# The third LSTM by seven block products, single groups by seven products too, and nine work tiles

## The chip, the cores and the metric

The kernel runs on one core of one Trainium2 chip. The metric is the device time of one execution in microseconds (us). The engines of the core are TensorE (PE, matmuls; PEld is its loading of weights), VectorE (DVE), ScalarE (ACT), GpSimd (POOL) and SyncE (SP), which here only issues transfers. All arithmetic is in f32.

## The reference, cut to what matters

The input is `x` of 128 x 64 x 256 (128 graphs of 64 nodes, 256 features) with one 64 x 64 adjacency matrix. Four layers follow one another, each with a residual and a layer norm: three graph convolutions; a spectral layer with the eigenvectors of the graph's Laplacian; a layer with two graph convolutions and four LSTMs; and a masked attention. The change is in the four LSTMs of the third layer:

```python
for p in range(1, MAX_SKIP + 1):                 # p = 1, 2, 3, 4
    nw = Tv // p                                 # 64 // p windows of p nodes
    wins = h[:, :nw * p, :].reshape(Bv * nw, p, Hd)
    last = _lstm_last(Wih[p - 1], Whh[p - 1], bih[p - 1], bhh[p - 1], wins)
    idx = jnp.arange(nw) * p + (p - 1)
    h = h.at[:, idx, :].set(last.reshape(Bv, nw, Hd))
```

One step of an LSTM is `x_t @ Wih.T + h @ Whh.T + bias`, four gates i, f, g, o of 256 features each, then `c = sigmoid(f) * c + sigmoid(i) * tanh(g)` and `h = sigmoid(o) * tanh(c)`. The first step has h = 0 and c = 0, so it needs neither `Whh` nor the gate f. LSTM p works on windows of p nodes and replaces the last node of each, so LSTM 3 sees what LSTM 2 wrote, and LSTM 4 what LSTM 3 wrote.

## The kernel before

**Groups and units.** The 128 graphs are 16 groups of eight graphs, 512 rows of 256 features each. Layer 0 (the first part, up to about 845 us) runs over all groups first, with the eigenvectors computed beside it. The other three layers then run group by group. `unit` (L1663) is the work of a unit: the first twelve groups make six units of two groups (pairs), the last four (`SINGLE = 4`) one unit each. `UNITS = 4` units are under way at a time.

**The planner.** Layers 1 to 3 are written as notes to a planner, `Plan` (L104). Each note is an operation (or a few matmuls) on one engine with a cost in us; `Plan.run` (L164) keeps a clock for each engine and emits the operation that can start first, among those within 0.02 us the one with the earliest due time. The due time is the group's number times `PERIOD` less the longest remaining chain of the operation. That sets the order of instructions on each engine, which then is fixed. The cost of a matmul is given in `products` (L1237): 1.673 ns a moving column plus 3 ns, at least 0.223 us. All instructions are issued in one helper, L162, so the profile puts them on that line, and they are told apart by tiles.

**Tiles.** Buffers come from named sets of slots: eight PSUM banks (`ps`), `WIDE` = 7 work tiles `w` of 1024 columns, `NARROW` = 3 of 512 (`v`), `GATES` = 6 gate tiles of 1024 columns, `CELLS` = 3 for the cell state `c`, `OUTS` = 4 for `hs`, the output handed to the next step. A tile is taken when its first operation is emitted and comes free when its last one is done. `Plan.MOST` (L112) tells how many slots are kept for the oldest unit.

**The LSTMs.** `to_lstm` (L1320) makes `hT`, the group's 512 rows with features on the partitions, as two `w`-sized halves k of 64 nodes x 8 graphs. A gate's weights are 256 x 256: two contraction halves k by two output halves h, so 128 x 128 blocks.

- `lstm` (L1483) is the direct form: for every gate and output half it sums over k the products of a 128 x 128 block and n moving columns, n being 8 graphs x number of windows. With p = 3 it has n = 8 x 21 = 168, with p = 4 n = 8 x 16 = 128. A first step has 3 gates x 2 halves x 2 = 12 matmuls, a later one 4 x 2 x 4 = 32.
- `fast` (L1540) is the form with seven products: the moving columns are cut in two halves w of n columns each, so that a gate is a product of 2 x 2 blocks, and seven products of blocks stand for the eight (Winograd's form of Strassen's method). A first step has 7 x 3 = 21 matmuls of n columns, a later one 7 x 4 x 2 = 56, where the direct form would have 24 and 64 of n columns. It needs four sums of weight blocks, made once by `add_weights` (L1216) on DVE into tiles `sums`, four sums of moving blocks per input (T1 to T4, on DVE, in a `w` tile), and three copies (ACT) and three additions (DVE) from PSUM in each pass over the gates. If (number of gates) x n is over 512, the gates are done in two passes of two. `quarters` (L1209) gives the four blocks of the weights.

LSTM 1 (`singles`, n = 256) and LSTM 2 (`pairs`, n = 128) use `fast` for every group, the halves being the first and last 32 nodes. LSTM 3 is `lstm(hT, 3, 0, 21)` for every group. LSTM 4 is `four` for a pair (L1648, n = 128, the halves being the two groups), and `lstm(hTs[0], 4, 0, 16)` for a single group.

The three lines that say which form LSTM 4 takes:

```python
        if len(groups) == 2:
            four(hTs)
        else:
            lstm(hTs[0], 4, 0, 16)
```

Of the kernel before, what the change touches and what calls it, by code (L numbers as in the profile page):

```python
# [11 lines left out]
F32 = mybir.dt.float32  # L12
AF = mybir.ActivationFunctionType
ALU = mybir.AluOpType
# [738 lines left out]
P = 128  # L753
D = 256
# [3 lines left out]
WIDE = 7  # L758
# [3 lines left out]
CELLS = 3  # L762
OUTS = 4
LASTS = 3
PERIOD = 17.0
# [62 lines left out]
def kernel(  # L828
# [25 lines left out]
    nc = tc.nc  # L854
# [6 lines left out]
    def tl(pool, shape, tag, **kw):  # L861
        uid[0] += 1
        return pool.tile(shape, F32, tag=tag, name=f"{tag}_{uid[0]}", **kw)
# [11 lines left out]
    def load(pool, name, src, pattern, shape, **kw):  # L875
        t = pool.tile(shape, F32, name=name)
        nc.sync.dma_start(t, src.rearrange(pattern, **kw))
        return t
# [88 lines left out]
    def run(out, pairs):  # L967
        for i, (lhsT, rhs) in enumerate(pairs):
            mm(out, lhsT, rhs, i == 0, i == len(pairs) - 1)
# [204 lines left out]
    wih, whh = [], []  # L1174
    for i in range(4):
        wih.append(load(wb, f"wih{i}", c_ih[i], "(k p) f -> p k f", [P, 2, 1024], p=P))
        whh.append(load(wb, f"whh{i}", c_hh[i], "(k p) f -> p k f", [P, 2, 1024], p=P) if i else None)
# [31 lines left out]
    def quarters(w):  # L1209
        w = w.rearrange("p k (q h m) -> p k q h m", q=4, h=2)  # L1210
        return [w[:, k, :, h] for h in range(2) for k in range(2)]

    ways = {}
    SPARE21 = {(1, 0), (2, 0), (2, 1)}

    def add_weights(p, ready):  # L1216
        ways[p] = []
        names = "igo" if p == 1 else "ifgo"
        for k, w in enumerate((wih[p - 1], whh[p - 1])):
            if w is None:  # L1220
                continue
            spare21 = (p, k) in SPARE21
            s = wb.tile([P, 4 - spare21, len(names), P], F32, name=f"sums{p}{k}")
            s, w = plan.tile("sums", [P, 4 - spare21, len(names), P], s), plan.tile("sums", [P, 2, 1024], w)
            whole = quarters(w)
            for at, to in ((slice(0, 1), slice(0, 1)), (slice(2, 4), slice(1, 3))) if p == 1 else ((slice(0, 4),) * 2,):
                a11, a12, a21, a22 = (x[:, at] for x in whole)
                S1, S2, S4, S3 = [s[:, j, to] for j in range(4 - spare21)] + [a21] * spare21
                V.tensor_add(S1, a21, a22, ready=ready)
                V.tensor_sub(S2, S1, a11, ready=ready)  # L1230
                V.tensor_sub(S4, a12, S2, ready=ready)
                V.tensor_sub(S3, a11, a21, ready=ready)
            raw = [{q: x[:, "ifgo".index(q)] for q in names} for x in whole]
            sums = [{q: s[:, j, i] for i, q in enumerate(names)} for j in range(4 - spare21)] + [raw[2]] * spare21
            ways[p].append([raw[0], raw[1], raw[3], sums[0], sums[1], sums[3], sums[2]])

    def products(calls, also=(), **kw):  # L1237

        size = lambda x: x.at.size if isinstance(x, Part) else int(np.prod(x.shape[1:]))
        cost = sum(max(0.001673 * size(c[2]) + 0.003, 0.223) for c in calls)  # L1240
        plan.note("PE", [("matmul", (o, l, r), {"start": a, "stop": z, **kw}) for o, l, r, a, z in calls], cost,
                  also=also)
# [8 lines left out]
    def work():  # L1251
        return plan.tile("w", [P, 1024])
# [4 lines left out]
    def ps4(shape=(P, 512)):  # L1257
        return plan.tile("ps", shape)
# [61 lines left out]
    def to_lstm(xs, there):  # L1320
# [20 lines left out]
        lstm(hT, 3, 0, 21)  # L1341
# [141 lines left out]
    def lstm(hT, p, first, nw):  # L1483

        n = 8 * nw
        wi, wh, bias = wih[p - 1], whh[p - 1], cbi[:, p - 1, :]
        hs = None
        for t in range(p):  # L1490
            rows = slice(first + t, first + t + (nw - 1) * p + 1, p)
            xt = [hT[:, k, rows, :] for k in range(2)]
            last = t == p - 1
            names = "figo" if t else "igo"
            gate = []
            for h in range(2):
                G = plan.tile("gates", [P, 1024])[:, :len(names) * n].rearrange("p (q n) -> p q n", n=n)
                gate.append({q: G[:, i] for i, q in enumerate(names)})
            if not t:
                c = plan.tile("c", [P, 512])[:, :2 * n].rearrange("p (h n) -> p h n", h=2)  # L1500
            new = None if last else plan.tile("hs", [P, 512])[:, :2 * n].rearrange("p (h n) -> p h n", h=2)
            for h in range(2):
                for q in names:
                    j = 2 * "ifgo".index(q) + h
                    m = slice(j * P, (j + 1) * P)
                    pp = ps4()[:, :n]
                    ins = [(wi[:, k, m], xt[k]) for k in range(2)]
                    outs = [(wh[:, k, m], hs[:, k, :]) for k in range(2)] if t else []
                    if t and h == 0 and q in names[:2]:

                        run(pp, ins, last=False)
                        run(pp, outs, first=False)
                    else:
                        run(pp, ins + outs)
                    S.activation(gate[h][q], pp, AF.Tanh, bias=bias[:, j:j + 1], scale=0.5 if q == "g" else 0.25)
                    if q == "g":
                        to = gate[h]["g"] if t else c[:, h, :]
                        if t:
                            V.scalar_tensor_tensor(c[:, h, :], gate[h]["f"], 1.0, c[:, h, :], op0=ALU.add,
                                                   op1=ALU.mult)  # L1520
                        V.scalar_tensor_tensor(to, gate[h]["i"], 1.0, gate[h]["g"], op0=ALU.add,
                                               op1=ALU.mult)
                        if t:
                            V.scalar_tensor_tensor(c[:, h, :], c[:, h, :], 0.5, to, op0=ALU.mult, op1=ALU.add)
                        S.activation(gate[h]["i"], c[:, h, :], AF.Tanh, scale=0.5)
                    if q == "o" and not last:
                        V.scalar_tensor_tensor(new[:, h, :], gate[h]["o"], 1.0, gate[h]["i"], op0=ALU.add,
                                               op1=ALU.mult)
            if p == 4 and t == 2:
                plan.late = plan.ops[-1]  # L1530
            if last:

                for h in range(2):
                    V.scalar_tensor_tensor(hT[:, h, slice(first + p - 1, first + nw * p, p), :],
                                           gate[h]["o"].rearrange("p (w b) -> p w b", b=8), 1.0,
                                           gate[h]["i"].rearrange("p (w b) -> p w b", b=8), op0=ALU.add,
                                           op1=ALU.mult)
            hs = new

    def fast(p, n, x, hs=None, c=None, new=None, write=None):  # L1540
# [8 lines left out]
        def parts(v):  # L1549
            return v.rearrange("p (r b) -> p r b", b=8)  # L1550
# [11 lines left out]
        T = work()[:, :4 * n * len(ins)].rearrange("p (s i n) -> p s i n", s=len(ins), i=4)  # L1562
        T1, T2, T3, T4 = ([parts(T[:, s, i]) for s in range(len(ins))] for i in range(4))
# [60 lines left out]
    def state(tag):  # L1624
        return plan.tile(tag, [P, 512]).rearrange("p (h w n) -> p h w n", h=2, w=2)

    def turn_out(dst, o, t):
        V.scalar_tensor_tensor(dst, o.rearrange("p (r b) -> p r b", b=8), 1.0, t.rearrange("p (r b) -> p r b", b=8),
                               op0=ALU.add, op1=ALU.mult)
# [18 lines left out]
    def four(hTs):  # L1648

        def write(h, o, t):  # L1650
            for w in range(2):
                turn_out(hTs[w][:, h, 3:64:4, :], o[:, w], t[:, w])

        c, hs = state("c"), None
        for t in range(4):
            x = [[hTs[w][:, k, t:t + 61:4, :] for w in range(2)] for k in range(2)]
            new = state("hs") if t < 3 else None
            fast(4, 128, x, hs, c, new, write)
            if t == 2:
                plan.late = plan.ops[-1]  # L1660
            hs = new

    def unit(groups):  # L1663

        if groups[0] == 0:
            add_weights(1, 10.0)
            add_weights(2, 30.0)
            add_weights(4, 60.0)
# [17 lines left out]
        if len(groups) == 2:  # L1686
            four(hTs)
        else:
            lstm(hTs[0], 4, 0, 16)
# [11 lines left out]

    spare[0] = lambda: tl(few, [P, D], "spare")
# [56 lines left out]
```

## Time and profile before

| What | Value |
|---|---|
| median of 3 runs | 2364.02 us (2361.47 to 2365.95) |
| the profiled execution's own time | 2365.63 us |
| its span, first to last instruction | 2363.8 us |
| TensorE clock granted, mean | 0.992 |
| PE busy | 2313.2 us (98%), 19872 matmul passes |
| PEld busy | 2035.5 us (86%), 19872 weight loads |
| DVE busy | 1630.6 us (69%), 5562 instructions |
| ACT busy | 1137.4 us (48%), 2838 instructions |
| POOL busy | 142.8 us (6%) |
| PE's share of the chain that ended last | 92% |

A busy PE is not PE at its peak, since the lengths of matmuls overlap. The lines of a group read: line, engine, operation, output tile <- inputs (moving, then weights), shape of the weights, shape of the moving data, count | busy us, mean ns | idle time of the engine before them, and who ended it.

### The profile page before, as it was taken

The page shows a single profiled execution, that of the slowest core. Times are in us where ns is not written, and L with a number is a line of the kernel's source. Part 1 is how long each engine was busy: PE and PEld are TensorE (multiplying, and loading weights), DVE is VectorE, ACT ScalarE, POOL GpSimd, SP SyncE. Part 2 cuts the span into 40 slices and gives each one's busy share as a digit, 9 for nine tenths or more (in the row PEclk, how much of TensorE's full clock was granted, in tenths as well). Part 3 has the DMA queues.
Part 4 walks back from the last instruction along what each step waited for, and adds up shares of the span by engine and source line. Part 5 has one row for each costly group of instructions (what it writes and reads, how often), then busy time and mean ns, then how long its engine had stood idle before and what let it go on. Part 6 is the DMA issues. An engine that isn't in the chain of part 4 may idle for free.

```text
span 2363.8 us, 50357 instructions
## 1 busy us (share of the span) xinstructions
PE 2313.2 (98%) x19872; PEld 2035.5 (86%) x19872; DVE 1630.6 (69%) x5562; ACT 1137.4 (48%) x2838; POOL 142.8 (6%) x315
## 2 busy tenths in 40 slices
PE   8999999999999999999999999999999999999996
PEld 6877888887787778999899899899999998998995
DVE  6888887778898557558567666756755858567535
ACT  2333343333333346555546545545556455545544
POOL 0000000000000010001000100100000101011002
PEclk9999999999999999999999999999999999999998
DMA  7000000000000040002111211220210312222001
GB/s 236 10 1 10 19 10 10 10 10 10 11 10 10 1 161 13 16 11 72 54 42 55 81 51 39 80 65 32 81 43 32 120 48 66 66 92 84 19 1 48
DMA packets 79837, 108.08 MB, mean 46 GB/s; under 512 B 23280, under 2 KB 63984, under 8 KB 79600
## 3 DMA queue, kind: packets, MB, share of 16 engines
q1 hardware_dynamic: 79248, 104.58, 13.3%
q8 instruction: 156, 2.56, 0.4%
q14 instruction: 81, 0.66, 0.1%
q10 hardware_dynamic: 352, 0.28, 0.0%
HBM read 57.90 MB, written 45.09 MB: 44 GB/s over the span
## 4 chain that ended last, share of the span: by engine, by line
PE 92%; DVE 5%; ACT 1%; issue 1%; POOL 0%; DMA 0%; SPq 0%; ACTq 0%; POOLq 0%; DVEq 0%
PE ps L162 60%; PE ps L963 30%; PE ps L1006 2%; DVE D L52 1%; DVE X L162 1%; PE pc L312 1%; DVE w L162 1%; DVE tw L52 0%; DVE st L162 0%; POOL rs L162 0%; DVE gates L162 0%; ACT gates L162 0%; DVE ss L52 0%; DVE v L162 0%; DMA XA<-in_x_dram 0%
## 5 line engine op out<-in xcount | busy, mean ns | idle before, releaser
L162 PE MATMUL ps<-w,wih 128*128 128x128 f32 (+2 forms) x3708 | 649.7, 299 | 3.2 <-DVE gates L162 1.7
L162 PEld LDWEIGHTS ps<-w,wih 128*128 128x128 f32 x3708 | 550.6, 191 | 33.0 <-issue 13.6
L162 ACT ACTIVATE gates<-ps,cbi 128x168 f32<-128x168 f32 (+2 forms) x722 | 261.5, 388 | 207.7 <-PE ps L162 204.1
L162 PE MATMUL ps<-w,sums 128*128 128x128 f32 (+1 forms) x2368 | 353.8, 289 | 3.0 <-ACT gates L162 2.0
L162 PE MATMUL ps<-hs,whh 128*128 128x128 f32 (+1 forms) x1952 | 343.2, 291 | 1.4 <-DVE hs L162 1.4
L162 PEld LDWEIGHTS ps<-w,sums 128*128 128x128 f32 x2368 | 307.6, 192 | 16.6 <-issue 4.3
L162 PEld LDWEIGHTS ps<-hs,whh 128*128 128x128 f32 x1952 | 288.3, 191 | 3.2 <-DVE hs L162 1.8
L162 ACT ACTIVATE gates<-gates,cbi 128x256 f32<-128x256 f32 (+2 forms) x500 | 214.3, 477 | 129.1 <-DVE gates L162 129.0
L162 DVE TENSOR_TENSOR gates<-gates,ps 128x512 f32<-128x512 f32 (+2 forms) x264 | 157.5, 601 | 164.1 <-PE ps L162 157.1
L963 PE MATMUL ps<-aw,h 128*128 128x256 f32 x1024 | 228.2, 380 | 0.0
L963 PEld LDWEIGHTS ps<-aw,h 128*128 128x128 f32 x1024 | 192.6, 190 | 25.9 <-issue 0.4
L162 ACT COPY gates<-ps 128x512 f32<-128x512 f32 (+2 forms) x264 | 136.8, 520 | 160.6 <-PE ps L162 158.8
L972 ACT ACTIVATE h<-h 128x512 f32<-128x512 f32 x128 | 80.6, 630 | 184.4 <-DVE h L52 184.2
L162 DVE SCALAR_TENSOR_TENSOR gates<-gates 128x256 f32<-128x256 f32 (+3 forms) x188 | 78.4, 418 | 69.9 <-ACT gates L162 69.6
L963 PE MATMUL ps<-aw,m 128*128 128x512 f32 x256 | 120.5, 612 | 0.9 <-ACT m L1010 0.9
L963 PE MATMUL ps<-m,aw 128*128 128x256 f32 x512 | 119.7, 387 | 1.0 <-ACT LV L385 0.6
L963 PE MATMUL ps<-ss,tw 128*128 128x256 f32 x512 | 117.8, 379 | 0.1
L963 PE MATMUL ps<-ss,aw 128*128 128x256 f32 x512 | 116.7, 379 | 0.0
L963 PEld LDWEIGHTS ps<-m,aw 128*128 128x128 f32 x512 | 98.1, 194 | 17.3 <-issue 3.0
L162 DVE SCALAR_TENSOR_TENSOR c<-gates,c 128x256 f32<-128x256 f32 (+2 forms) x156 | 56.6, 363 | 76.8 <-ACT gates L162 76.4
L963 PEld LDWEIGHTS ps<-ss,aw 128*128 128x128 f32 x512 | 96.8, 190 | 13.0
L162 POOL TENSOR_SCALAR rs<-mv 128x2 f32<-128x2 f32 x96 | 23.7, 256 | 1390.8 <-DVE mv L162 1372.1
(326 smaller groups left out, 3559.2 us busy)
## 6 DMA issues: line engine op xcount, KB each, us to landing
far<-w SPq DMA_DIRECT2D x42, 512.0 KB, 2.7
w<-far SPq DMA_DIRECT2D x168, 128.0 KB, 3.0
X<-rest SPq DMA_DIRECT2D x24, 512.0 KB, 3.3
out_dram<-X SPq DMA_DIRECT2D x64, 128.0 KB, 1.8
rest<-XA SPq DMA_DIRECT2D x12, 512.0 KB, 2.6
rest<-X SPq DMA_DIRECT2D x12, 512.0 KB, 2.8
XA<-in_x_dram SPq DMA_DIRECT2D x22, 256.0 KB, 6.0
wih<-in_c_ih_dram SPq DMA_DIRECT2D x4, 1024.0 KB, 7.7
```

What stands on the lines that cost most here:

```text
L52: return getattr(self.engine, name)(out, *args, **kw)
L162: getattr(e, name)(*[real(x) for x in args], **{k: real(v) for k, v in kw.items()})
L312: PE.matmul(out, lhsT, rhs, start=True, stop=True)
L963: PE.matmul(out, lhsT, rhs, start=start, stop=stop)
L972: S.activation(dst, src, AF.Relu)
L1006: PE.matmul(p[h][m, k, t, :], src[hs, t, f], sqT2[hs, hs], start=True, stop=True)
```

## The change

LSTM 3 goes to `fast` too, and LSTM 4 does so for single groups. A new function `long` takes the place of `four` and serves both LSTMs and both kinds of unit: for a pair the halves are the two groups; for a single group they are windows 0 to 7 and 8 to 15 (p = 4), or graphs 0 to 3 and 4 to 7 (p = 3, where 21 windows can't be halved). n is 64 // p x 4 for each group of the unit: 168 and 128 for a pair, 84 and 64 for a single group. `lstm` goes away. LSTM 3 leaves `to_lstm` and runs in `unit` when all the unit's groups have come through LSTM 2.

`add_weights` makes sums for p = 3 too. The fourth weight sum of every LSTM now overwrites the block a21 that it is made from, so a `sums` tile holds three. LSTM 1's weights are loaded in the order i, g, o without f, in two transfers. A `fast` step whose T1 to T4 do not fit in one `w` tile takes two. The spare output of the norms left over from layer 0 goes to a part of the `sums` tile of LSTM 4. The slots become `WIDE` 9, `CELLS` 2 (state tiles are 672 columns instead of 512), `OUTS` 2, `PERIOD` is 18, and the planner's cost of a matmul 1.673 ns a column + 10 ns, without a least value.

```diff
-WIDE = 7
+WIDE = 9
 NARROW = 3
 GATES = 6
 ATT = 2
-CELLS = 3
-OUTS = 4
+CELLS = 2
+OUTS = 2
 LASTS = 3
-PERIOD = 17.0
+PERIOD = 18.0
...
-        wih.append(load(wb, f"wih{i}", c_ih[i], "(k p) f -> p k f", [P, 2, 1024], p=P))
+        if i:
+            wih.append(load(wb, f"wih{i}", c_ih[i], "(k p) f -> p k f", [P, 2, 1024], p=P))
+        else:
+            wih.append(wb.tile([P, 2, 768], F32, name="wih0"))
+            for to, at, n in ((0, 0, 256), (256, 512, 512)):
+                nc.sync.dma_start(wih[0][:, :, to:to + n],
+                                  c_ih[0].rearrange("(k p) f -> p k f", p=P)[:, :, at:at + n])
...
+            nq = len(names)
+            s = wb.tile([P, 3, nq, P], F32, name=f"sums{p}{k}")
+            if p == 4:
+                spare[0] = lambda s=s: s[:, 0, 0:2, :].rearrange("p q n -> p (q n)")
+            s, w = plan.tile("sums", [P, 3, nq, P], s), plan.tile("sums", [P, 2, nq * 2 * P], w)
+            a11, a12, a21, a22 = whole = quarters(w)
+            S1, S2, S4 = (s[:, j] for j in range(3))
+            V.tensor_add(S1, a21, a22, ready=ready)
+            V.tensor_sub(S2, S1, a11, ready=ready)
+            V.tensor_sub(S4, a12, S2, ready=ready)
+            V.tensor_sub(a21, a11, a21, ready=ready)
...
-        cost = sum(max(0.001673 * size(c[2]) + 0.003, 0.223) for c in calls)
+        cost = sum(0.001673 * size(c[2]) + 0.01 for c in calls)
...
-        lstm(hT, 3, 0, 21)
         return hT
...
-        T = work()[:, :4 * n * len(ins)].rearrange("p (s i n) -> p s i n", s=len(ins), i=4)
-        T1, T2, T3, T4 = ([parts(T[:, s, i]) for s in range(len(ins))] for i in range(4))
+        if 4 * n * len(ins) <= 1024:
+            T = work()[:, :4 * n * len(ins)].rearrange("p (s i n) -> p s i n", s=len(ins), i=4)
+            T = [T[:, s] for s in range(len(ins))]
+        else:
+            T = [work()[:, :4 * n].rearrange("p (i n) -> p i n", i=4) for _ in ins]
+        T1, T2, T3, T4 = ([parts(v[:, i]) for v in T] for i in range(4))
...
-    def state(tag):
-        return plan.tile(tag, [P, 512]).rearrange("p (h w n) -> p h w n", h=2, w=2)
+    def state(tag, n=128):
+        return plan.tile(tag, [P, 672])[:, :4 * n].rearrange("p (h w n) -> p h w n", h=2, w=2)
...
-    def four(hTs):
+    def long(hTs, p):
+
+        def seen(h, w, t):
+            if len(hTs) == 2:
+                return hTs[w][:, h, t:t + 64 // p * p - p + 1:p, :]
+            if p == 4:
+                return hTs[0][:, h, 32 * w + t:32 * w + t + 29:4, :]
+            return hTs[0][:, h, t:t + 61:3, 4 * w:4 * w + 4]
 
         def write(h, o, t):
             for w in range(2):
-                turn_out(hTs[w][:, h, 3:64:4, :], o[:, w], t[:, w])
...
+                turn_out(seen(h, w, p - 1), o[:, w], t[:, w])
+
+        n = 64 // p * 4 * len(hTs)
+        c, hs = state("c", n), None
+        for t in range(p):
+            x = [[seen(k, w, t) for w in range(2)] for k in range(2)]
+            new = state("hs", n) if t < p - 1 else None
+            fast(p, n, x, hs, c, new, write)
...
+            add_weights(3, 45.0)
             add_weights(4, 60.0)
...
-        if len(groups) == 2:
-            four(hTs)
-        else:
-            lstm(hTs[0], 4, 0, 16)
+        for p in (3, 4):
+            long(hTs, p)
```

## The prediction

> **What bounds the kernel now.** I read four views in this order: busy time by stage, PE's waits, the weight loads by shape, and PE's order in time.
>
> Busy time by stage (span, then PE, weight loads, DVE, ACT, POOL in us with instructions, PE clock, DMA share, GB/s):
>
> ```profile
> 900.00:1200.00 300.00, 300.00 (x2666) 281.96 (x2665) 185.24 (x484) 170.84 (x426) 13.82 (x24) 1.00 0.10 33
> 1800.00:2100.00 300.00, 296.06 (x2597) 275.70 (x2597) 205.59 (x576) 166.20 (x419) 22.46 (x44) 0.99 0.21 68
> 2200.00:2300.00 100.00, 100.00 (x777) 98.06 (x776) 40.98 (x119) 54.23 (x156) 0.00 (x0) 1.00 0.02 6
> 2300.00:2364.00 64.00, 45.02 (x355) 38.32 (x353) 34.97 (x125) 29.74 (x76) 12.15 (x36) 0.86 0.14 44
> ```
>
> Layers 1 to 3 run from about 845 us. Up to 2300 PE is full; DVE reaches at most 69% of a stage. The same table has DVE at 901 us of the 1400 between 900 and 2300. PE's waits in those 1400 us (who, for whom, us, times, longest):
>
> ```profile
> PE ps L162 <- ACT gates L162: 2.0, 3, 0.7
> PE ps L162 <- DVE gates L162: 1.7, 1, 1.7
> PE ps L162 <- ACT w L162: 1.6, 3, 0.5
> PE ps L162 <- DVE hs L162: 1.4, 2, 0.9
> PE ps L162 <- ACT v L162: 0.7, 1, 0.7
> PE ps L162 <- DVE w L162: 0.6, 1, 0.6
> ```
>
> That is 8.0 us in all. So the change is worth what it does to the sum of PE's own work, and better buffering can give back about 8 us there at most. What one matmul costs PE is not its duration (they are pipelined) but the distance from its start to the next one's. Each f32 matmul appears as two passes, each with its own weight load: the five groups of LSTM matmuls (3708 + 2368 + 1952 + 400 + 272) make 8700 passes, twice the 4350 that I count in the code. PE's order in time (start, length of the merged run):
>
> ```profile
> 2233.87 5.29 PE L162 MATMUL ps<-w,wih 128*128 128x168 f32 x36
> ...
> 908.47 3.74 PE L162 MATMUL ps<-w,sums 128*128 128x128 f32 x32
> ...
> 2317.47 1.47 PE L162 MATMUL ps<-ident,w 128*128 128x128 f32 x12
> ...
> 524.76 0.27 PE L312 MATMUL pc<-de,eig_c 64*64 64x1 f32 x2
> ```
>
> Take the last one's own length off and divide by the gaps. 168 columns: (5.29 - 0.306)/35 = 142.4 ns. 128 columns: (3.74 - 0.275)/31 = 111.8 ns; the commonest distance between starts is 111 to 112, so I use 111.6. Between 256 columns starts lie 215.8 ns apart. From 168 to 256 the slope is 0.833 ns a column, and 168 x 0.833 + 2.5 is 142.5. The same line gives 109.2 at 128. The transposes, also 128 columns, do run at (1.47 - 0.273)/11 = 108.8. The ordinary 128-column pass is 2.4 ns above it. The weight loads by shape (count, busy us, mean ns) say why:
>
> ```profile
> L162 PEld LDWEIGHTS ps<-w,wih 128*128 128x128 f32 x3708 | 550.6, 191 | 33.0 <-issue 13.6 <-DVE gates L162 3.1 <-PE ps L162 1.7
> ...
> L162 PEld LDWEIGHTS ps<-w 128*64 128x64 f32 x512 | 17.5, 137 | 6.5 <-ACT w L162 2.3 <-ACT v L162 2.3 <-issue 0.8
> ...
> L162 PEld LDWEIGHTS ps<-ident,w 128*128 128x128 f32 x32 | 3.5, 141 | 0.7 <-ACT w L162 0.5
> ```
>
> 64 weight columns more take 191 - 137 = 54 ns more: a 128-column load occupies the array for about 107 ns (191 includes some 84 of latency). Transposes load faster (141) and keep to the line; ordinary passes of 128 columns stand just above 107. I read this as a floor: each pass needs the next weights loaded during the present one, so no 128-weight pass is shorter than 111.6 ns, however few columns move. The last row of the order in time agrees in kind: with ONE moving column the two passes start about 0.08 us apart (0.27 less a duration of 0.19 to 0.20), though one column should stream in 3 ns.
>
> **The change part by part.**
>
> *Third LSTM, pairs of groups (six pairs).* Before: 76 matmuls of 168 columns per group, 152 per pair. After: seven products instead of eight, still of 168 columns: 21 + 56 + 56 = 133. That is 19 x 6 = 114 matmuls fewer at 2 x 142.5 ns: **-32.5 us**. This is full gain, because PE is the bound and 168 columns lie above the floor.
>
> *Third LSTM, the four single groups.* The halves are now four batches each, so a product moves 21 x 4 = 84 columns: 133 matmuls of 84 instead of 76 of 168. By the streaming line a pass would be 72.5 ns; by the floor 111.6. Floor: (133 x 223.2 - 76 x 285) ns x 4 = (29.7 - 21.7) x 4 = **+32.1 us**. Line: (19.3 - 21.7) x 4 = -9.5.
>
> *Fourth LSTM, single groups.* 108 matmuls of 128 become 21 + 3 x 56 = 189 of 64. Floor: (42.2 - 24.1) x 4 = **+72.3 us**. Line (55.8 ns a pass): (21.1 - 24.1) x 4 = -12.
>
> No row has 128 weight columns with fewer than 128 moving, so this price is bounded. From below by the line: all in all -54 us. From above by the one-column row: load of 53 plus 26 there, so 107 + 26 = 132 ns here. The passes are (133 + 189) x 4 x 2 = 2576; at 20.7 ns more each, +53, all in all +125. I take 111.6, from the nearest row: same weight shape, same overlapped stream. The total of these three is **+71.9 us**. One number decides the sign: with 2576 passes at p, against 2432 passes of 142.5 and 864 of 111.6 before (443 us) and 1596 of 142.5 kept (227.5), break-even is p = 83.7 ns.
>
> On this the Trainium skill has two sections of "TensorE: Matmul & The Clock Gate". "Back-to-back issue gap" gives an isolated matmul N/2.4 + 2.5 ns, with only a small issue floor under 64 columns; doubled for two cycles a column that is the line, and by it the sum would be -54. "LDWEIGHTS (loading the stationary operand)" charges columns/1.2 whatever the rows, 106.7 ns here, and the former section adds that in streams of load and matmul both set the spacing; by that the sum would be 2576 x 106.7 + 227.5 - 443 = +59. The second speaks against this change, and the rows above side with it.
>
> *DVE and ACT.* DVE rows (128 columns 283 ns, 168: 328, 256: 418, 512: 684) are about 0.15 us + 1.05 ns a column. Third LSTM of a pair after: 20 operand sums of 168 (6.6 us), 3 additions from PSUM of 504 and 12 of 336 (8.0), cell work 18 of 336 and 4 of 168 (10.3): 24.9 against 40 x 0.328 = 13.1, so +11.8 x 6 = 71 us. A single: +9.0 for the third, +10.8 for the fourth, x 4 = 79. DVE goes from 901 to about 1050 us of some 1470, 71%; ACT (768 us) gains the copies from PSUM, some 60 us. Both lie beside a full PE: 0. If that cover is gone, the price is rival 3's.
>
> *Weights.* Three sums per weight instead of three or four; the fourth overwrites the quarter it is taken from, which no direct LSTM reads any more. The third LSTM adds 8 DVE operations of 512 columns (5.5 us); the first drops from 8 small ones to 4 (-0.6). In the trace such sums run at 910 to 918 while PE is full with other groups. If that cover failed, 5 us; at best -1; I take +1. The first weight loads as two transfers of 768 KB in all instead of one of 1 MB on SP: one more issue, 0.25 MB less, among 7 MB loaded: 0.
>
> *Buffers and order.* Nine w tiles instead of seven, cells 3 to 2, outputs 4 to 2, PERIOD 18, and a planner cost of 0.01 + 1.673 ns a column, which takes a 64-column matmul for 0.117 us instead of 0.223. An underpriced PE only makes PE later than planned; others then wait for it. But a pair's third LSTM step now needs four of six gate tiles (two passes, each with a tile per half) and holds a cell and an output tile, with two of each for four units. The third LSTM also moves: from two chains, one behind each group's own pairs, to one chain that begins when both groups have come so far, with the fourth behind it; no DMA moves with it, and SP and POOL keep their orders. The ending of a step is exposed when no other unit is ready. Best -8 (all of PE's waits gone), worst +25; I take +3. The tail (2300 on) keeps its two waits of 5.5 and 5.4 us for ACT; -5 to +8, I take +2.
>
> Sum: 71.9 + 1 + 3 + 2 = +78. The profiled execution took 2365.6 us (span 2363.8, 1.8 around it), 1.6 above the median of 2364.0: 2365.6 + 78 - 1.6 = **2442 us**.
>
> **The rivals.**
>
> 1. *No weight floor; small matmuls stream at their columns.* For: nothing in the trace runs below 128 columns on full weights, and 2.4 ns is a thin sign. Against: transposes and the one-column row. -54 + 6 gives 2316. It decides below 83.7 ns a pass. Chance 0.10, of which 0.01 falls about at break-even.
> 2. *A short pass cannot overlap its load fully* (132 ns a pass): 71.9 + 53 + 6 gives 2495. For: the one-column row. Against: full-width passes do overlap. 0.07.
> 3. *Floor, and the tiles starve PE.* Ending of a pair step from rows: four ACT gates 1.6 us, four DVE operations of 336 about 2.0, ACT 0.5, four operand sums 1.3, some 5.5 us; 18 such steps, a third exposed: +33 us, 2472. For: four of six gate tiles. Against: 8 us of waits now, and three other units. 0.10.
>
> My own case has 0.73.
>
> **How the numbers follow.** A difference of 0.2% (4.7 us) is about what can be told from none. Faster is rival 1 less its share at break-even: 0.09; same 0.01; slower 0.90. The range leaves out rival 1 and the top of 2: from floor at 108 ns (the least distance seen between 128-column loads) and the best scheduling, 2410, to 2490. My own case's range is 2415 to 2465.
>
> **What would show it.** Right: passes of 84 and 64 columns start 111 to 112 ns apart, no nearer than those of 128; PE still full to the tail; about 876 more PE passes; the growth sits in the last four groups, while 12 groups in pairs gain some 32 us. Wrong: starts 56 and 73 ns apart (rival 1), 130 (rival 2), or PE waits beyond 30 us on gates and hs (rival 3).

## The result and the profile after

The changed kernel takes 2479.24 us (2477.65 to 2481.52), against 2362.74 us for the kernel before: 1.049 times as long, 95% interval 1.047 to 1.051. The prediction was 2442 us with a range of 2410 to 2490. The profiled execution took 2481.5 us, 115.9 more than that of before.

The page's rows of busy tenths in 40 slices of the span, with PE's clock, already show where to look:

```profile
PE   8999999999999999999999999999999999999997
PEld 6877888778777789999989989999998999899996
DVE  6887877768887486577688587697686764775414
...
PEclk9999999999999999999999999999999999999856
```

PE is full as before, but the granted clock (PEclk) falls in the last three slices. The busy time by stage (the same columns as in the prediction) shows where:

```profile
900.00:1200.00 300.00, 299.08 (x2713) 278.85 (x2712) 214.98 (x548) 179.98 (x431) 12.19 (x24) 1.00 0.10 33
1800.00:2100.00 300.00, 297.23 (x2738) 278.86 (x2737) 210.50 (x631) 156.69 (x411) 21.18 (x44) 1.00 0.22 70
2200.00:2300.00 100.00, 100.00 (x936) 93.61 (x932) 63.75 (x213) 57.11 (x162) 3.81 (x8) 1.00 0.16 50
2300.00:2340.00 40.00, 39.71 (x349) 39.36 (x347) 20.34 (x82) 15.37 (x54) 1.76 (x4) 1.00 0.07 18
2340.00:2440.00 100.00, 96.85 (x454) 96.45 (x454) 19.90 (x79) 22.86 (x82) 1.26 (x3) 0.51 0.00 1
2440.00:2480.00 40.00, 23.74 (x160) 17.78 (x160) 21.25 (x75) 19.23 (x48) 10.25 (x30) 0.76 0.08 27
```

From 2340 to 2440 PE is 97% busy and yet the clock is half (0.51): 454 passes in 100 us, where 349 took 40 us just before. PE's waits between 900 and 2300 us fell from 8.0 to 3.5 us:

```profile
PE ps L162 <- DVE w L162: 2.9, 3, 1.9
PE ps L162 <- ACT gates L162: 0.4, 1, 0.4
PE ps L162 <- DVE hs L162: 0.2, 1, 0.2
```

The floor of the prediction is the least distance between the starts of two passes that each load 128 weight columns. PE's order in time shows it, at full clock and then at half:

```profile
2300.76 1.95 PE L162 MATMUL ps<-w,sums 128*128 128x84 f32 x16
2302.55 0.37 PE L162 MATMUL ps<-w,wih 128*128 128x64 f32 x2
...
2325.70 3.74 PE L162 MATMUL ps<-w,sums 128*128 128x64 f32 x32
2329.27 0.39 PE L162 MATMUL ps<-w,wih 128*128 128x64 f32 x2
...
2347.13 3.62 PE L162 MATMUL ps<-w,sums 128*128 128x64 f32 x16
2350.54 0.64 PE L162 MATMUL ps<-w,wih 128*128 128x64 f32 x2
```

From the start of a run to the start of what follows it: 84 columns (2302.55 - 2300.76)/16 = 111.9 ns; 64 columns (2329.27 - 2325.70)/32 = 111.6 ns; 64 columns after the clock has fallen (2350.54 - 2347.13)/16 = 213.1 ns. So in a row of such passes 128, 84 and 64 columns all cost 111 to 112 ns at full clock. That is the floor. At half clock it nearly doubles: 448 of the 1512 passes of 64 columns lie 200 to 225 ns before the next one (444 of them in the stretch of half clock), and their excess over 111.6 ns adds up to 45.5 us. The forecast for PE's own work was +71.9. Together that is 117.4, against 115.9 measured; about -1.5 is left for buffers, weights and tail.

The floor belongs to a row of weight loads and not to the single pass. The first narrow pass behind wider ones is shorter:

```profile
1965.83 1.03 PE L162 MATMUL ps<-w,sums 128*128 128x256 f32 x4
1966.70 0.79 PE L162 MATMUL ps<-w,wih 128*128 128x84 f32 x6
1967.33 1.09 PE L162 MATMUL ps<-w,sums 128*128 128x84 f32 x7
```

The six passes from 1966.70 to 1967.33 take 630 ns. Five at 111.6 leave 72 ns for one, which is the streaming line (72.5 ns at 84 columns); in the trace it is the first. In the whole kernel 78 of the 2576 narrow passes lie under 105 ns from the next one, down to 72 ns at 84 columns and 55 ns at 64, and every one of them stands directly behind a wider pass. A least time of the pass itself would hold for these too.

Where the clock falls, PE's order shows one wait of 1.1 us, for the output of the step before (`hs`), in the middle of 64-column passes:

```profile
2339.10 0.39 PE L162 MATMUL ps<-w,whh 128*128 128x64 f32 x2
2339.32 0.39 PE L162 MATMUL ps<-w,wih 128*128 128x64 f32 x2
2340.83 0.53 PE L162 MATMUL ps<-hs,whh 128*128 128x64 f32 x2 [1.12 <-DVE hs L162]
2341.15 0.64 PE L162 MATMUL ps<-w,wih 128*128 128x64 f32 x2
```

The half clock then lasts from 2341.0 to 2446.8, until wider passes come. Theory A: what grants the clock looks at how much of the time columns stream through the array. By the prediction's 0.833 ns a column a 64-column pass streams 53 of 111.6 ns at full clock and, as an estimate with twice that, 107 of 213 at half; that is too little to bring the clock back. Theory B: the doubled distance is a property of such small passes (how they read memory, or waits that the trace doesn't show), or the single wait alone did it.

### The profile page after: what moved, and what is told of

It reads as the page before. It is cut to its first block, busy times and chain, and to the rows that moved or that the text cites. A ratio compares the mean times of both kernels' runs of the same rounds, so it can differ in the third digit from the quotient of the medians.

```text
span 2479.7 us, 52787 instructions
## 1 busy us (share of the span) xinstructions
PE 2431.1 (98%) x20748; PEld 2151.2 (87%) x20748; DVE 1753.6 (71%) x5960; ACT 1194.9 (48%) x3014; POOL 141.3 (6%) x315
## 4 chain that ended last, share of the span: by engine, by line
PE 93%; DVE 4%; issue 1%; ACT 1%; DMA 0%; POOL 0%; SPq 0%; ACTq 0%; POOLq 0%; DVEq 0%
PE ps L162 62%; PE ps L963 29%; PE ps L1006 2%; DVE D L52 1%; PE pc L312 1%; DVE w L162 1%; DVE tw L52 0%; DVE X L162 0%; DVE gates L162 0%; POOL rs L162 0%; DMA aw<-in_a_w_dram 0%; DVE st L162 0%; ACT gates L162 0%; DVE ss L52 0%; DVE c L162 0%
## 5 line engine op out<-in xcount | busy, mean ns | idle before, releaser
L162 PE MATMUL ps<-w,wih 128*128 128x128 f32 (+4 forms) x3360 | 648.7, 298 | 1.3 <-ACT gates L162 0.7
L162 PE MATMUL ps<-w,sums 128*128 128x128 f32 (+4 forms) x3576 | 550.7, 296 | 3.2 <-DVE w L162 3.2
L162 PEld LDWEIGHTS ps<-w,sums 128*128 128x128 f32 x3576 | 488.9, 198 | 20.3 <-issue 6.6
L162 DVE TENSOR_TENSOR gates<-gates,ps 128x512 f32<-128x512 f32 (+5 forms) x438 | 239.9, 555 | 289.9 <-PE ps L162 276.6
L162 ACT ACTIVATE gates<-gates,cbi 128x256 f32<-128x256 f32 (+6 forms) x840 | 335.1, 455 | 182.1 <-DVE gates L162 179.6
L162 ACT COPY gates<-ps 128x512 f32<-128x512 f32 (+5 forms) x438 | 209.8, 482 | 344.8 <-PE ps L162 342.4
L162 PE MATMUL ps<-hs,whh 128*128 128x128 f32 (+3 forms) x1056 | 218.1, 290 | 1.5 <-DVE hs L162 1.4
L162 PE MATMUL ps<-w,whh 128*128 128x128 f32 (+3 forms) x1056 | 218.0, 289 | 0.0
L162 PEld LDWEIGHTS ps<-w,whh 128*128 128x128 f32 x1056 | 170.9, 200 | 0.0
L162 ACT ACTIVATE gates<-ps,cbi 128x128 f32<-128x128 f32 (+4 forms) x420 | 129.1, 369 | 44.0 <-PE ps L162 42.7
```

What stands on the lines that cost most here:

```text
L162: getattr(e, name)(*[real(x) for x in args], **{k: real(v) for k, v in kw.items()})
```

## The experiments

### 1. The 64-column passes padded to 128

```diff
+        twice = n == 64
...
-                    calls.append((bank[:, j, :], ways[p][s][weight[i]][q], moving[i][s], new and not calls,
+                    rhs = moving[i][s]
+                    if twice:
+                        rhs = rhs.unsqueeze(1).to_broadcast([P, 2] + list(rhs.at.shape))
+                    calls.append((bank[:, j], ways[p][s][weight[i]][q], rhs, new and not calls,
...
-            shape = (P, len(qs), n)
+            shape = (P, len(qs), 2, n) if twice else (P, len(qs), n)
```

> The changed kernel with every 64-column pass given its moving columns twice (128 columns into 128 columns of PSUM, the second half never read); the planner is charged as for 64, so the order of instructions is the same. Floor theory: at full clock a pass stays 111.6 ns, so the padding costs nothing in itself. If the clock fell because too small a part of each pass streams (53 of 111.6 ns), the padded passes hold it at 1.00 and the time falls by about 45 us to 2434. If the clock fell for the one wait of 1.3 us or for anything else than the columns, half clock stays and the time is 2479. If the doubled distance comes from how such small passes read memory and not from the clock, padding makes it longer: over 2479. If there is no floor and 64-column passes are slow for another reason, 2479 or more.

Measured: 2435.72 us (2435.03 to 2436.24), 1.031 times the kernel before (1.029 to 1.032). So streaming each column twice makes the kernel some 44 us faster than the changed one. PE's order has the same wait at nearly the same place, and the passes behind it:

```profile
2338.23 0.39 PE L162 MATMUL ps<-w,wih 128*128 128x128 f32 x2
2339.74 0.49 PE L162 MATMUL ps<-hs,whh 128*128 128x128 f32 x2 [1.12 <-DVE hs L162]
...
2343.19 1.95 PE L162 MATMUL ps<-w,sums 128*128 128x128 f32 x16
2344.98 0.39 PE L162 MATMUL ps<-w,wih 128*128 128x128 f32 x2
```

(2344.98 - 2343.19)/16 = 111.9 ns, with twice the columns. And by stage:

```profile
2340.00:2390.00 50.00, 50.00 (x450) 50.00 (x450) 16.43 (x64) 19.84 (x70) 0.00 (x0) 1.00 0.00 1
```

450 passes in 50 us, at clock 1.00. The floor is shown (64 and 128 columns cost the same), and theory B falls: the wait alone does not do it, since it is there and the clock stays, and the doubled distance goes with the granted clock. A is what is left: four executions with padding have a mean clock of 0.991 to 0.993, four without it 0.972 or 0.973. Which quantity of the streaming is counted, columns or time, is not shown. 2435.7 is 71.2 above the kernel before in the same job, as the sum of 71.9 had it.

### 2. The third LSTM or the fourth alone in the single groups

The fourth weight sum keeps a place of its own for the LSTM that is done directly, and `lstm` is back for it. The extra sum takes memory, so both kernels have eight work tiles instead of nine. For the fourth direct (the third by seven products):

```diff
-WIDE = 9
+WIDE = 8
...
+            ns = 4 if p in (4,) else 3
+            s = wb.tile([P, ns, nq, P], F32, name=f"sums{p}{k}")
...
-            V.tensor_sub(a21, a11, a21, ready=ready)
+            S3 = s[:, 3] if ns == 4 else a21
+            V.tensor_sub(S3, a11, a21, ready=ready)
...
         for p in (3, 4):
-            long(hTs, p)
+            if len(hTs) == 1 and p in (4,):
+                lstm(hTs[0], p, 0, 64 // p)
+            else:
+                long(hTs, p)
```

> As the changed kernel, but single groups do the fourth LSTM directly (eight work tiles). So the third has passes of 84 columns, and none has 64. Floor theory: -32.5 + 32.1, about 2362 us. Clock: an 84-column pass streams 70 of its 111.6 ns, and if that is enough to hold the clock, it stays at 1.00 up to the tail; if any pass under the floor lets it fall, half clock shows and the time is 2380 or more. Streaming theory without a floor: 2321.

Measured: 2382.06 us, 1.008 (1.006 to 1.009). Some 20 us above what the floor gives, so 84 columns are not safe either. PE waits 2.2 us behind 84-column passes, and the clock is half from 2264.7 to 2292.0:

```profile
2264.32 0.46 PE L162 MATMUL ps<-w,wih 128*128 128x128 f32 x2 [2.24 <-DVE w L162]
...
2269.20 3.62 PE L162 MATMUL ps<-w,sums 128*128 128x84 f32 x16
2272.62 0.63 PE L162 MATMUL ps<-w,wih 128*128 128x84 f32 x2
```

(2272.62 - 2269.20)/16 = 213.8 ns a pass at half clock. 27.3 us at half clock cost at most 13.7. What made the rest is not shown: PE's waits from 900 to 2300 are 8.9 us and those behind them 10.3 (one of 8.0), near the 8.0 and 11.6 of the kernel before. The half clock ends as 28 passes of 128 columns come.

The other way round (`p in (3,)` in place of `(4,)`):

> As the changed kernel, but single groups do the third LSTM directly (eight work tiles), so the 64-column passes of the fourth are the only ones under 128. Floor theory: -32.5 + 72.3, about 2403 us with the clock held, and up to 2448 if the clock halves over the last 64-column passes as in the changed kernel. If the half clock needs the 84-column passes too, 2403.

Measured: 2433.81 us, 1.028 (1.022 to 1.033). Between the two values, and the runs tell why: three took 2433.5 to 2437.4 with a mean clock of 0.981 or 0.982, the fourth 2410.7 with 0.993. The profiled one has the half clock from 2339.1 to 2386.9, after a wait of 0.7 us among 64-column passes, and most of that stretch is one row of the stages:

```profile
2340.00:2386.00 46.00, 46.00 (x214) 45.82 (x214) 5.88 (x20) 9.05 (x33) 0.00 (x0) 0.50 0.00 0
```

So whether the clock falls there differs from run to run, and it is worth some 24 us; with it held the time is within 8 of the 2403 that the floor gives.

### 3. Only the pairs changed, with seven work tiles and with nine

The third experiment's first form does both LSTMs of single groups directly (`p in (3, 4)` in the diff above). The four sums then take more memory, so the work tiles went down to seven:

> Only pairs of groups take the seven products in the third LSTM; single groups do the third and fourth directly, as before (the fourth weight sum of these two LSTMs has its own place again, and the work tiles go back to seven for that). Floor theory: 114 matmuls of 168 columns fewer at 285 ns, -32.5 us, about 2330 us; the clock stays at 1.00 up to the tail, since no pass has 64 columns. If the buffers or the order starve PE in the pairs (rival 3), over 2345. If the seven products gain nothing, 2363.

Measured: 2403.51 us, 1.017 (1.016 to 1.019), 73 us above the forecast. PE's waits between 900 and 2300:

```profile
PE ps L162 <- DMA att<-v: 26.6, 3, 12.6
PE ps L162 <- DMA w<-far: 12.8, 2, 8.3
PE ps L162 <- ACT v L162: 5.4, 1, 5.4
PE ps L162 <- DVE w L162: 4.8, 4, 2.0
```

The whole list makes 59.9 us, where the kernel before has 8.0: starvation, of which the prediction had only a mild form, by gates and state tiles. To tell work tiles from cells, outputs and gates, the next kernel keeps nine tiles and restores the overwritten blocks when the single groups begin (`plain` holds the weight tiles, which `lstm` reads):

```diff
+        if groups[0] == NT // 4 - SINGLE:
+            for p in (3, 4):
+                for w in plain[p]:
+                    a11, a12, a21, a22 = quarters(w)
+                    V.tensor_sub(a21, a11, a21)
...
         for p in (3, 4):
-            long(hTs, p)
+            if len(hTs) == 1:
+                lstm(hTs[0], p, 0, 64 // p)
+            else:
+                long(hTs, p)
```

> As the first experiment, single groups do the third and fourth LSTM directly, but with nine work tiles: the overwritten weight blocks are restored by four operations of 512 columns on DVE when the single groups begin. If the 60 us of waits for transfers in the first experiment came from its seven work tiles, they go, and the pairs' saving shows: 2364.5 - 32.5 = about 2332 us with the clock held. If they came from the two cell and two output tiles, the gates or the order, which are the same here, they stay: about 2400.

Measured: 2332.14 us, 0.987 (0.985 to 0.989); 30.4 less than the kernel before, of 32.5 forecast. PE's waits up to 2260 are 7.4 us:

```profile
PE ps L162 <- DVE w L162: 5.7, 6, 1.5
PE ps L162 <- DVE gates L162: 1.2, 2, 0.8
PE ps L162 <- DVE hs L162: 0.5, 1, 0.5
```

So the seven products pay in pairs, and with nine work tiles two cells, two outputs and four of six gate tiles leave PE no more waits than before.

### 4. Fewer single groups

The last kernel with `SINGLE = 2`:

> The same with only the last two groups single and direct, and groups 12 and 13 a seventh pair: one pair more saves 19 x 0.285 = 5.4 us in the third LSTM and 2 x 24.1 - 42.2 = 6.0 us in the fourth. Floor theory: 2321 us, if the shorter run of single groups still fills PE to the tail; if it doesn't, between 2321 and 2345.

Measured: 2328.88 us, 0.986 (0.984 to 0.987): 3.3 less than with four single groups, of 11.4 in PE's sum. Most of that saving doesn't reach the end. Up to 2260 us PE waits 10.2 us instead of 7.4, and the mean clock is 0.989 instead of 0.993. Between 900 and 2260 us the clock is half from 1992.6 to 1999.4 and from 2098.4 to 2101.8, where the kernel with four single groups has it full; 10.2 us at half clock cost about 5. The two together make up most of the missing 8.1 us.

The changed kernel itself, with no single group:

```diff
-SINGLE = 4
+SINGLE = 0
```

> The changed kernel with no single group, so all eight pairs have products of 168 and 128 columns and no pass lies under the floor. By PE's sum: 8 x 5.4 + 2 x 6.0 = 55.3 us less than before, 2309 us. Against it: at the end one chain of seven steps is alone, and the ending of a step (some 5.5 us by the durations of before) is exposed up to seven times, +38 us and more if the clock falls in these gaps: 2309 to 2355. If the loss of the changed kernel had nothing to do with the narrow passes, it stays near 2479.

Measured: 2320.65 us, 0.982 (0.981 to 0.984): the fastest of all, 42 us faster than the kernel before and 159 faster than the changed one, which differs by this one number. PE's waits from 900 to 2260 are 13.4 us:

```profile
PE ps L162 <- DVE hs L162: 5.1, 4, 2.1
PE ps L162 <- DVE gates L162: 4.6, 4, 1.5
PE ps L162 <- DVE w L162: 3.1, 2, 2.4
```

Of the 55 us by PE's sum 42 arrive. Most of the waits above fall behind 2200: up to there PE waits 5.3 us. In the tail PE is idle 6 us longer (118.0 - 92.6 = 25.4 us from 2200 to 2318, against 64.0 - 45.0 = 19.0 from 2300 on before), far less than the 38 that I had given the lone chain. What takes the rest of the missing 13 us is not shown.

Finally the same with `WIDE = 7` in place of 9 and nothing else changed, to price the nine work tiles alone:

> The all-pairs kernel with seven work tiles instead of nine, and nothing else changed. If the waits of the first experiment (60 us, mostly for transfers behind work tiles) came from the work tiles alone, PE waits 40 to 70 us more here than with nine: 2361 to 2391. If nine tiles make no difference and the waits there had another cause, about 2321.

Measured: 2425.52 us, 1.025 (1.024 to 1.027): 105 us more than with nine tiles (102 if each is set against the kernel before of its own job), beyond the range I gave. PE's waits from 900 to 2300, the first of a list that makes 84.3 us:

```profile
PE ps L162 <- DMA att<-v: 32.8, 3, 12.8
PE ps L162 <- DMA w<-far: 27.4, 3, 17.1
PE ps L162 <- DVE w L162: 7.5, 8, 1.7
PE ps L162 <- DVE gates L162: 5.3, 6, 1.1
```

The stages tell what the 105 us are made of. First the kernel with seven work tiles, then the one with nine:

```profile
900.00:2300.00 1400.00, 1315.31 (x11722) 1200.64 (x11714) 973.48 (x2590) 756.90 (x1815) 81.34 (x164) 0.97 0.17 54
900.00:2200.00 1300.00, 1294.44 (x11722) 1194.57 (x11721) 968.88 (x2595) 763.33 (x1816) 86.37 (x164) 1.00 0.18 58
```

The same number of passes (11722) takes 1400 us with seven and 1300 with nine. PE is idle for 84.7 us against 5.6, so 79 us are waits. It is busy for 1315.3 us against 1294.4, so 21 us are slower passes: the clock is 0.97 on average, half in five stretches of 10 to 21 us around the long waits. PE stands behind the attention's transfers with no other unit ready to fill in. That the units lack work tiles follows from the edit; which tile is missing at each wait I did not trace.

## Why the prediction was right or wrong

**The bound.** Right: PE stayed full, and PE's own sum decided, at the clock that was granted. DVE at 71% of the span and ACT at 48% cost next to nothing: PE waited 3.5 us from 900 to 2300. Two readings of the prediction are slightly off and change nothing: before, DVE reaches 71% in the stage 2100 to 2200 and not 69% at most, and 107 + 26 makes 133 ns and not 132, 2 us more for rival 2.

**The floor.** Right in size, and to the digit in a row of narrow passes. From 2.4 ns between an ordinary 128-column pass and the line, and from loads 54 ns longer for 64 columns more, I had 111.6 ns for any pass with 128 weight columns. Measured: 111.9 at 84 and 111.6 at 64. The rivals of 56 and 73 ns (streaming) and 132 ns (load not overlapped) are out. "No 128-weight pass is shorter than 111.6 ns, however few columns move" was too strict: 78 passes, each directly behind a wider one, are shorter. So the reason given, the next weights' load, holds, and it is a limit on a row of loads. The one-column row, on 64 x 64 weights, was a sign of the right kind and no measure.

The page "TensorE: Matmul & The Clock Gate" of the Trainium skill, section "LDWEIGHTS (loading the stationary operand)", was the right one of the two rules weighed: by its 106.7 ns the sum was +59, by the row +71.9, and the measured 71.2 goes with the row.

**The three LSTM terms.** -32.5 for the pairs: 30.4 measured with the rest of the change in place. The sum of +71.9: 71.2 measured when the clock is held. The third and fourth alone came out at +48 and +100 against the kernel with both direct (each set against the kernel before of its job), instead of 32.1 and 72.3. Each has a stretch of half clock, worth at most 13.7 us and some 24; each also has eight work tiles instead of nine, whose part was not measured.

**The tail: the step that was left out.** "The tail (2300 on) keeps its two waits of 5.5 and 5.4 us for ACT; -5 to +8, I take +2." The waits did stay (12.1 us for those of 2300 to 2480), but I priced every narrow pass at full clock. So the 64-column passes of the term +72.3 were mis-sized: 444 of them ran at half clock, and the part left out measured 45.5 us. The rows of before held a hint that I passed over: the clock there is 0.86 in 2300 to 2364, so waits in the tail lower it. What no row of before showed is that narrow passes, which leave PE busy, then keep it low. The same page of the Trainium skill, "Part 1: The HAM clock gate", has the clock come back after one busy window of about 3.4 us. The lengths of the stretches fit such windows: by the page's 3.413 us, an estimate, 105.8 us are 31 of them, 47.8 are 14 and 27.3 are 8. But PE was 96% busy over the 31 (101.5 of 105.8 us) and the clock did not come back. Here the measurement decides, and by the padded run busy is better read as columns streamed. The number 2442 was low by 37 us, and 2479 lies above 2465, the top of the range for my own case. The wider range had room only because it reached toward rival 2, which is another mechanism; that it held is luck.

**Buffers and order.** As a total right: the remainder is about -1.5 where I had +6 with weights and tail; the terms in it were not measured one by one. Rival 3 (starvation) did not come. But "at best -8" misjudged what nine work tiles are for: the new form needs them, and without them the all-pairs kernel loses 105 us.

**Which groups.** Right: the loss sits in the four single groups. Take those away and the same change is a gain of 1.8%.

## What to carry to other kernels

Before a product is cut into more and smaller ones, find the columns below which a matmul pass no longer gets shorter: compare the distance between starts with the line through the wider shapes, and with the length of a weight load. Below that point a saving in arithmetic can be a loss in time, and here padding up to it cost nothing. Then look at the granted clock next to the busy time: an engine full of narrow passes can be busy at half speed, and the wait of 1.1 us that cost no more among 128-column passes cost tens of us among 64-column ones. When a step is made to work on two units at once, check that its buffers grew with it before judging it.

## What the runs showed of the hardware that I had not expected

- PE 96% busy at half clock for 105.8 us (2341.0 to 2446.8), nearly all of it passes that stream 64 columns. The weight load slows with it: 333 ns each against 192, and 213.1 ns a pass against 111.6.
- A narrow pass directly behind a wider one goes at the streaming line (72 ns at 84 columns); the floor of 111.6 ns needs a row of loads.
- The state holds itself. 64-column passes ran for 17 us at full clock (2322 to 2339) and kept it; after one wait of 1.1 us they ran at half and did not get it back. In the kernel with the third LSTM alone, 84-column passes with a few of 128 did the same for 27.3 us. Padded to 128 columns, the same stream went through the same wait at 1.00.
- It differs between runs: with the fourth LSTM alone three runs had a mean clock of 0.98 and one had 0.993, 23 to 27 us faster.
- Where exactly between 84 and 128 columns a stream recovers, and how long a wait must be, was not measured; the shortest that stood ahead of such a stretch is 0.7 us.
